# Four changes to a transformer kernel on one core: a column maximum by transposes, merged values in weight rooms, bias tiles opened earlier, expert gates applied to the activations

## The chip, the core and the metric

The kernel runs on one core of a Trainium2 chip. The metric is the device time of one launch in microseconds (us); lower is better. The core has a matrix engine (TensorE, PE in the profile), a vector engine (VectorE, DVE), a scalar engine (ScalarE, ACT), a general engine (GpSimd, POOL) and a queue engine (SyncE, SP), each of which runs its own list of instructions in order and waits on semaphores set by the others. On-chip memory is SBUF; matrix products land in a small accumulator memory, PSUM, which PE writes and DVE and ACT read. Everything here is in 32-bit floats unless said otherwise.

## The reference

The input is x of 2 x 1024 tokens by 256, and a context of 2 x 77 by 256. Four layers follow; each is an attention over the context and a feed-forward part, each with a layer norm before it and a residual after it:

- layer 0: 16-head attention, then eight dense 256x256 experts of which the gate keeps two;
- layer 1: 16-head attention, then an int8 matrix product;
- layer 2: one-head attention with a norm, then eight gated experts of width 128, of which two count;
- layer 3: 16 heads of width 64 with rotary positions and a relative bias, then eight experts with 320 places each, and a shared path for tokens that found no place.

The parts that the change touches are these lines (shortened):

```python
# layer 1: int8 product; the scale of rhs is one number per column
rhs_scale = maximum(max(abs(rhs), axis=0), 1e-12) / 127
q_rhs = clip(round(rhs / rhs_scale), -127, 127)
x = x + (q_lhs @ q_rhs) * lhs_scale * rhs_scale
# layer 2: eight experts, combined with the gate's weights
for e in range(8):
    o = silu(xf @ gate_proj[e].T) * (xf @ up_proj[e].T) @ down_proj[e].T
    y = y + combine_w[:, e, None] * o
# layer 3: bias by distance, values, output projection
scores = Q @ K.T * scale + rel_pos_bias[:, |i - j|]
x = x + (softmax(where(mask, scores, -1e9)) @ V) @ Wo
```

## The kernel before

The 2048 tokens are four groups (G) of 512, and each group is four slices (J) of 128 tokens, one per partition. x stays in SBUF throughout. The stages run in this order: attention 0 (names ending in a0), feed-forward 0 (f0), attention 1 (a1), then for each group the int8 product (f1) and attention 2 (a2) as a list of nine steps called `chain`, feed-forward 2 (f2), attention 3 (a3) and feed-forward 3 (f3). The chain of groups 0 and 1 is called from within attention 1 (function `beside`), that of groups 2 and 3 from within the loops of f2 over groups 0 and 1. The preparation of attention 3 is a generator, `layer3_setup`, whose pieces are also called between the pieces of f2.

The order of the source is not the order on the engines. A planner, which simulates the program as it is built, may move an instruction ahead of others on its engine as long as data and buffers allow; SP, which issues nearly all DMAs, and POOL are in order at run time like the other engines. So an instruction that waits holds all behind it on its engine.

Large matrices live in six rooms of 8 KB per partition, used in turn (`weight`, pool "w"). A matrix is loaded when the last reader of the room's former tenant is done. PSUM is used through two double-bank tiles (`pbig`) and some single-bank ones.

**Int8 matrix (`layer1_ffn_setup`, L577 to L587).** The 256x256 matrix rhs is loaded into a room at the start, and POOL takes the maximum of its absolute values over all partitions with `partition_all_reduce` (L580). DVE takes the larger of the two halves (L582), scales it (L583), inverts it (L584), and `quantize` (L567 to L573) rounds the matrix. In POOL's list L580 stands in the middle of attention 0, between multiplies by 1/sum of the softmax (L419).

**Feed-forward 2 (`layer2_ffn`, L692 to L770).** `route` computes a group's gate weights cw, 128 tokens by 8 experts per slice. `hidden` makes one expert's activations for 512 tokens: eight PE instructions of gate and up (L745, pgu_f; a 32-bit product is two PE instructions), silu on ACT (L750), and the product with up on DVE (L751, hT_f). `down` multiplies a slice's activations by the eight down matrices (L758), each expert into its own part of PSUM, and DVE adds each to x times its gate (L765): eight such evictions of 128x256 per slice, 128 in all.

**Attention 3 (`layer3_setup`, `layer3_attention`, L795 to L1012).** The values are merged with the output projection: each of 8 pieces (two batches by four key heads) is computed in PSUM, copied to a tile vo3 by ACT and DVE, and written to a DRAM tensor vd3 (L877 is its DMA). `layer3_attention` opens its own pools when those of f2 are closed, loads the rotary tables cs (L888), reads the merged values back as vw (L897, L900), and for each of 16 slices loads a bias tile rb of 128 x 16 x 77 (L920), adds the mask to it on POOL (L924), makes queries (L930, pq_a), rotates them (L781, L785 on DVE, L791 on POOL), transposes them (L949), makes scores (L965), adds the bias (L972), and after the softmax transposes the weights (L1000) and multiplies by vw (L1007).

**Feed-forward 3.** Tokens are scattered by indirect DMAs on POOL to a DRAM buffer by expert and place. The experts' matrices w1 and w2 (1 MB each) are loaded into the six rooms (L1317, L1319).

Of the kernel before, what the change touches and what calls it, by code (L numbers as in the profile page):

```python
# [33 lines left out]
P = 128  # L34
# [32 lines left out]
def tile_layers(ctx: ExitStack, tc: tile.TileContext, a: dict, out: bass.AP):  # L67
# [71 lines left out]


# [354 lines left out]
    def layer0_ffn(mp):  # L495
# [16 lines left out]
        for g in range(G):  # L512
# [19 lines left out]
            for j in range(J):  # L532
                nc.tensor.transpose(pg[:, j * P : (j + 1) * P], gate[:, j, :], ident)
# [41 lines left out]
    def layer1_ffn_setup():  # L575
# [4 lines left out]
        nc.gpsimd.partition_all_reduce(am, rw, P, bass_isa.ReduceOp.absmax)  # L580
        rsc, rrs = room[:, 0, 2], room[:, 0, 3]
        nc.vector.tensor_tensor(rsc, am[:, 0, :], am[:, 1, :], ALU.max)  # L582
        nc.vector.tensor_scalar(rsc, rsc, 1e-12, 1.0 / 127.0, ALU.max, ALU.mult)  # L583
# [108 lines left out]
    def layer2_ffn_weights():  # L692
        wgu = []
        for nm in ("gate2T", "up2T"):
            t = weight([P, KC, E * INTER], nm)
            nc.sync.dma_start(t, a[nm].rearrange("(c p) n -> p c n", p=P))
            wgu.append(t)
        return wgu

    def layer2_ffn(fp, wgu):  # L700

        wd = weight([P, E, D], "down2T")
        nc.sync.dma_start(wd, a["down2T"].rearrange("e i h -> i e h"))
# [3 lines left out]
        xnTs, cws, hTs = {}, {}, {}  # L707

        def route(g):
# [18 lines left out]
            cws[g] = cw = st.tile([P, J, E], F32, tag="cw", name=f"cw_{n}")  # L728
# [5 lines left out]
            nc.vector.tensor_tensor(cw, cw, bc(tot, E), ALU.mult)  # L734

        def hidden(g, e):
            n = f"f2{g}"
            if e % 4 == 0:
                hTs[g, e // 4] = fp.tile(
                    [P, E // 2, GT], F32, tag="hT", name=f"hT_{n}{e}", bufs=3  # L740
                )
            pgu = pbig(f"pgu_{n}{e}")
            for i in range(2):
                for kc in range(KC):
                    nc.tensor.matmul(  # L745
                        pgu[:, i, :], wgu[i][:, kc, e * INTER : (e + 1) * INTER],
                        xnTs[g][:, kc, :], start=(kc == 0), stop=(kc == KC - 1),
                    )
            sg = fp.tile([P, GT], F32, tag="sg", name=f"sg_{n}{e}")
            nc.scalar.activation(sg, pgu[:, 0, :], AF.Silu)  # L750
            nc.vector.tensor_tensor(hTs[g, e // 4][:, e % 4, :], sg, pgu[:, 1, :], ALU.mult)  # L751

        def down(g, j):
            x = xs[g][:, j, :]
            for half in range(2):
                po = pbig(f"po_f2{g}{j}{half}")
                for e in range(4):
                    nc.tensor.matmul(  # L758
                        po[:, e // 2, (e % 2) * D : (e % 2) * D + D],
                        hTs[g, half][:, e, j * P : (j + 1) * P], wd[:, 4 * half + e, :],  # L760
                        start=True, stop=True,
                    )
                for e in range(4):
                    ee = 4 * half + e
                    nc.vector.scalar_tensor_tensor(  # L765
                        x, po[:, e // 2, (e % 2) * D : (e % 2) * D + D],
                        cws[g][:, j, ee : ee + 1], x, ALU.mult, ALU.add,
                    )

        return route, hidden, down  # L770


# [22 lines left out]
    def layer3_setup():  # L795
# [67 lines left out]
        for b, vT in enumerate(vTs):  # L863
            vd = dp.tile([H * L, D], F32, name=f"vd3{b}")
            for g4 in range(KV):
                rows = slice(g4 % 2 * HD3, g4 % 2 * HD3 + HD3)
                vo = ap.tile([L, H // KV, D], F32, tag="vo3", name=f"vo3{b}{g4}")
# [14 lines left out]
        yield wq, mb3, kblk, vds  # L882

    def layer3_attention(route, wq, mb3, kblk, vds):
        with tc.tile_pool(name="a3", bufs=2) as ap, tc.tile_pool(name="a3c", bufs=1) as c3:
            cs = c3.tile([P, 2, 2, J, HD3], F32, name="cs")
# [6 lines left out]
            vws = []  # L893
            for b, vd in enumerate(vds):
                vw = c3.tile([P, NC3, D], F32, name=f"vw3{b}")
                full = (NC3 - 1) * P
                nc.sync.dma_start(  # L897
                    vw[:, : NC3 - 1, :], vd[:full, :].rearrange("(m p) n -> p m n", p=P)
                )
                nc.sync.dma_start(vw[: H * L - full, NC3 - 1, :], vd[full:, :])  # L900
                vws.append(vw)
# [14 lines left out]
            def queries(it):  # L916
                g, j = divmod(it, J)
                n, gb = f"a3{g}{j}", g % 2
                rb = ap.tile([P, H, L], F32, tag="rb", name=f"rb_{n}")
# [70 lines left out]
            def values(it):  # L990
# [15 lines left out]
                for m, w in chunks:  # L1006
                    nc.tensor.matmul(  # L1007
                        po, t[:w, m, :], vws[g // 2][:w, m, :], start=(m == 0), stop=(m == NC3 - 1)
                    )
# [350 lines left out]
    with tc.tile_pool(name="masks", bufs=1) as mp:  # L1360
# [13 lines left out]
        with (  # L1374
# [4 lines left out]
            def beside(it):  # L1379
# [4 lines left out]
                for g in range(2):  # L1384
                    k = it - (g + 1) * J + 1
                    if 0 <= k < len(chain):
                        chain[k](g)

# [8 lines left out]
            gate_up = layer2_ffn_weights()  # L1397
            layer1_attention(weights, beside)
            with tc.tile_pool(name="a3s", bufs=2) as sp, tc.tile_pool(name="f2", bufs=2) as fp:
                route, hidden, down = layer2_ffn(fp, gate_up)  # L1400
                setup.send(sp)


                route(0)
                for g in range(G):
                    pieces = [lambda e=e: hidden(g, e) for e in range(E)]
                    pieces += [lambda j=j: down(g, j) for j in range(J)]
                    for k, piece in enumerate(pieces):
# [84 lines left out]
```

## Time and profile before

| | |
|---|---|
| median of 3 runs | 1149.47 us (1144.49 to 1151.27) |
| profiled execution | 1150.59 us, its span 1148.7 us |
| mean granted PE clock | 0.952 of full |
| PE, DVE, ACT, POOL busy | 1029.8, 719.4, 362.1, 386.3 us |
| DMA moved | 74.89 MB, 65 GB/s on average |
| chain that ended last | PE 56%, DVE 24%, DMA 7%, ACT 4%, POOL 4% |

The stages overlap; by PE's first and last instruction of each they lie about at: a0 0 to 175 us, f0 157 to 310, a1 283 to 460, f2 462 to 709, a3 709 to 925, the end of the routing 925 to 952, f3 952 to 1149.

A row of the profile's timeline gives the start, the duration, the engine, the source line, the operation, output and inputs by the program's names, sizes, and in brackets how long the engine had been idle and what released it. "issue" there means that the engine waited for nothing that the profile shows. A row of the groups gives busy us, mean ns of one instruction, and the idle time before it with its releaser. The slices cut the span in 40 parts of 28.7 us; digits are tenths.

### The profile page before, as it was taken

The page shows a single profiled execution, that of the slowest core. Times are in us where ns is not written, and L with a number is a line of the kernel's source. Part 1 is how long each engine was busy: PE and PEld are TensorE (multiplying, and loading weights), DVE is VectorE, ACT ScalarE, POOL GpSimd, SP SyncE. Part 2 cuts the span into 40 slices and gives each one's busy share as a digit, 9 for nine tenths or more (in the row PEclk, how much of TensorE's full clock was granted, in tenths as well). Part 3 has the DMA queues.
Part 4 walks back from the last instruction along what each step waited for, and adds up shares of the span by engine and source line. Part 5 has one row for each costly group of instructions (what it writes and reads, how often), then busy time and mean ns, then how long its engine had stood idle before and what let it go on. Part 6 is the DMA issues. An engine that isn't in the chain of part 4 may idle for free.

```text
span 1148.7 us, 13916 instructions
## 1 busy us (share of the span) xinstructions
PE 1029.8 (90%) x4770; PEld 645.5 (56%) x4770; DVE 719.4 (63%) x1848; ACT 362.1 (32%) x1115; POOL 386.3 (34%) x368
## 2 busy tenths in 40 slices
PE   5499999999998987897998999899899958999996
PEld 3255554444444444455655546577678844766774
DVE  5567965776578898949586547677878731222211
ACT  1457640000076563131231110555355521111100
POOL 5443320112343544423120000675566641121211
PEclk9699998999999898898999999999999987999998
DMA  8400008245200000111102004523042323253630
GB/s 269 57 3 1 1 23 165 38 82 88 80 1 1 1 1 1 39 48 31 40 23 59 1 1 161 145 45 67 23 103 51 90 83 96 77 165 101 200 131 17
DMA packets 100279, 74.89 MB, mean 65 GB/s; under 512 B 57916, under 2 KB 90476, under 8 KB 100206
## 3 DMA queue, kind: packets, MB, share of 16 engines
q1 hardware_dynamic: 92974, 58.20, 18.3%
q10 hardware_dynamic: 4800, 9.46, 4.8%
q0 software_dynamic: 2432, 6.31, 1.6%
q8 instruction: 40, 0.66, 0.2%
q14 instruction: 33, 0.27, 0.1%
HBM read 55.35 MB, written 19.64 MB: 65 GB/s over the span
## 4 chain that ended last, share of the span: by engine, by line
PE 56%; DVE 24%; DMA 7%; ACT 4%; issue 4%; POOL 4%; SPq 0%; POOLq 0%; DVEq 0%; ACTq 0%
PE pe_f L545 10%; PE pgu_f L745 8%; PE poe_e L1273 4%; PE ph_e L1253 4%; PE po_a L1007 4%; DMA out_x<-ye_e,ids_e 3%; PE pq_a L930 3%; DVE x L765 3%; PE pc_a L450 3%; DVE x L156 2%; PE po_f L758 2%; PE pPT_a L437 2%; DVE mx_a L410 2%; DMA xe_e<-buf 2%; DVE sm_a L417 2%
## 5 line engine op out<-in xcount | busy, mean ns | idle before, releaser
L412 ACT ACTIVATE s_a<-psc_a,mx_a 128x77 f32<-128x77 f32 x512 | 121.5, 337 | 58.5 <-DVE mx_a L410 52.1
L419 POOL TENSOR_TENSOR s_a<-s_a,sm_a 128x616 f32<-128x616 f32 x64 | 78.3, 1223 | 123.9 <-DVE sm_a L418 89.4
L545 PE MATMUL pe_f<-ew,xnT_f 128*128 128x512 f32 x256 | 117.1, 607 | 0.0
L551 DVE SCALAR_TENSOR_TENSOR x<-pe_f,gate_f,x 128x256 f32<-128x256 f32 x128 | 61.8, 483 | 43.3 <-PE pe_f L545 40.7
L981 ACT ACTIVATE s_a<-s_a,mx_a 128x77 f32<-128x77 f32 x256 | 67.2, 347 | 61.4 <-DVE mx_a L979 61.2
L545 PEld LDWEIGHTS pe_f<-ew,xnT_f 128*128 128x128 f32 x256 | 48.3, 195 | 55.0 <-issue 53.0
L1007 PE MATMUL po_a<-vw,PT_a 128*128 128x256 f32 (+1 forms) x320 | 77.3, 381 | 0.8 <-ACT PT_a L1002 0.8
L1253 PE MATMUL ph_e<-xT_e,w 128*128 128x320 f32 x256 | 75.6, 436 | 0.0
L758 PE MATMUL po_f<-down2T,hT_f 128*128 128x256 f32 x256 | 65.0, 400 | 8.8 <-DVE x L765 8.7
L437 PE MATMUL pPT_a<-cst,s_a 128*128 128x128 f32 (+1 forms) x320 | 55.0, 292 | 17.8 <-POOL vr_a L343 11.5
L410 DVE TENSOR_REDUCE mx_a<-psc_a 128x4 f32<-128x308 f32 x128 | 57.9, 466 | 18.6 <-PE psc_a L401 11.4
L1077 DVE TENSOR_SCALAR hT_e<-ph_e,b1c 128x320 f32<-128x320 f32 (+1 forms) x36 | 20.6, 572 | 75.3 <-PE ph_e L1253 75.3
L930 PE MATMUL pq_a<-wq,xnT_a 128*128 128x512 f32 x128 | 60.5, 610 | 4.7 <-DVE s_a L972 4.7
L745 PE MATMUL pgu_f<-xnT_f,gate2T 128*128 128x512 f32 x128 | 63.5, 619 | 1.0 <-DVE hT_f L751 0.6
L765 DVE SCALAR_TENSOR_TENSOR x<-po_f,cw_f,x 128x256 f32<-128x256 f32 x128 | 60.8, 480 | 5.7 <-PE po_f L758 2.5
L437 PEld LDWEIGHTS pPT_a<-cst,s_a 128*128 128x128 f32 (+1 forms) x320 | 35.9, 143 | 49.5 <-issue 17.9
L1007 PEld LDWEIGHTS po_a<-vw,PT_a 128*128 128x128 f32 (+1 forms) x320 | 57.8, 190 | 9.6 <-issue 1.4
L1075 ACT ACTIVATE hT_e<-ph_e,b1c 128x320 f32<-128x320 f32 (+1 forms) x36 | 19.6, 545 | 138.0 <-PE ph_e L1253 138.0
L1273 PE MATMUL poe_e<-w,hT_e 128*128 128x256 f32 x256 | 61.3, 381 | 0.0
L758 PEld LDWEIGHTS po_f<-down2T,hT_f 128*128 128x128 f32 x256 | 48.3, 197 | 22.7 <-DVE x L765 15.4
L450 PE MATMUL pc_a<-PT_a,vblk_a 128*32 128x256 f32 (+1 forms) x512 | 57.2, 400 | 4.2 <-DVE PT_a L445 2.2
L745 PE MATMUL pgu_f<-xnT_f,up2T 128*128 128x512 f32 x128 | 60.1, 592 | 0.0
(311 smaller groups left out, 1979.8 us busy)
## 6 DMA issues: line engine op xcount, KB each, us to landing
w<-in_L_ffn_w SPq DMA_DIRECT2D x16, 1024.0 KB
rb_a<-in_relbias SPq DMA_DIRECT2D x16, 616.0 KB
buf<-none ACTq DMA_DIRECT2D x12, 769.5 KB
vd<-vo SPq DMA_DIRECT2D x8, 308.0 KB
vw<-vd SPq DMA_DIRECT2D x2, 1152.0 KB
xe_e<-buf SPq DMA_DIRECT2D x8, 257.0 KB
x<-in_x SPq DMA_DIRECT2D x4, 512.0 KB
ew<-in_L_ffn_expert_w SPq DMA_DIRECT2D x4, 512.0 KB
```

Source lines behind the costliest of these rows:

```text
L410: nc.vector.tensor_reduce(mx, sv, AX.X, ALU.min)
L412: nc.scalar.activation(s[:, c, 4 * i + h, :], sv[:, h, :], AF.Exp, bias=mx[:, h : h + 1], scale=-1.0,)
L437: nc.tensor.transpose(pt[: wide(m), m - m0, k * P : (k + 1) * P], sp[k][:, c, m * P : m * P + wide(m)], ident,)
L450: nc.tensor.matmul(pc[cols, c, :], vblk[g // 2][: wide(m), c, m, cols], t[: wide(m), m, :], start=(k == 0), stop=(k == 1),)
L545: nc.tensor.matmul(pe[:, i, :], xnT[:, kc, j * P : (j + 1) * P], ew[half][:, kc, i * 512 : (i + 1) * 512], start=(kc == 0), stop=(kc == KC ...
L745: nc.tensor.matmul(pgu[:, i, :], wgu[i][:, kc, e * INTER : (e + 1) * INTER], xnTs[g][:, kc, :], start=(kc == 0), stop=(kc == KC - 1),)
L758: nc.tensor.matmul(po[:, e // 2, (e % 2) * D : (e % 2) * D + D], hTs[g, half][:, e, j * P : (j + 1) * P], wd[:, 4 * half + e, :], start=Tr ...
L765: nc.vector.scalar_tensor_tensor(x, po[:, e // 2, (e % 2) * D : (e % 2) * D + D], cws[g][:, j, ee : ee + 1], x, ALU.mult, ALU.add,)
L930: nc.tensor.matmul(pq[:, i, :], xnTs[g][:, kc, j * P : (j + 1) * P], wq[:, kc, i * 512 : (i + 1) * 512], start=(kc == 0), stop=(kc == KC - 1),
L1007: nc.tensor.matmul(po, t[:w, m, :], vws[g // 2][:w, m, :], start=(m == 0), stop=(m == NC3 - 1))
L1253: nc.tensor.matmul(ph[:, h % 2, :rows], w1[:, kc, h * P : (h + 1) * P], xT[:, kc, :], start=(kc == 0), stop=(kc == KC - 1),)
L1273: nc.tensor.matmul(po, hT[:, h, i * P : (i + 1) * P], w2[:, h, :], start=(h == 0), stop=(h == NH - 1),)
```

## The change

Four parts, which share the SBUF and the rooms that they free or take.

1. **Maximum by transposes.** `partition_all_reduce` goes. PE transposes the matrix in four blocks, not before the gate transposes of f0's group 1 have been issued (`issue_after(gated[1])`); DVE takes the absolute maximum along the free axis and scales it; the result, copied along 128 columns, is transposed back by PE and copied by ACT.
2. **Merged values in weight rooms.** vw3 is no longer a tile of attention 3's pool: three weight rooms take its 18 chunks. They are loaded at the end of `layer3_setup`, that is, during f2. vo3 has one buffer instead of two.
3. **Bias tiles beside f2.** The pool of the bias tiles (a3c) is opened before f2's pools, so the first two tiles do not wait for f2's memory. In SP's list the loads of the first two stand right behind csk and m3; their mask additions stand in POOL's list among the first layer-2 attention steps of f2. The rotary tables move to the pool that opens after f2.
4. **Gates in the activations.** In f2, for groups 1 to 3, the gate weights are transposed by PE, copied by ACT, written to DRAM and read back once per expert as a tile cb in which all partitions hold the row of 512 gates. POOL multiplies silu's output by cb before DVE multiplies by up. The down products of all eight experts then accumulate in one PSUM tile, and DVE adds it to x once per slice. Group 0 keeps the former way. Its `route` is called from `beside`, and the loads of the router move with it.

With three rooms held by vw3 until attention 3 has used them, the first two experts' matrices of f3 are loaded later: w1_0 stands in SP's list between the bias loads rb_a322 and rb_a323, w2_0 before rb_a333, w1_1 behind it, w2_1 before the first load of tokens for f3.

```diff
+    gated = {}
...
-                nc.tensor.transpose(pg[:, j * P : (j + 1) * P], gate[:, j, :], ident)
+                turn_gate = nc.tensor.transpose(pg[:, j * P : (j + 1) * P], gate[:, j, :], ident)
+            gated[g] = turn_gate.ins
...
-        nc.gpsimd.partition_all_reduce(am, rw, P, bass_isa.ReduceOp.absmax)
         rsc, rrs = room[:, 0, 2], room[:, 0, 3]
-        nc.vector.tensor_tensor(rsc, am[:, 0, :], am[:, 1, :], ALU.max)
-        nc.vector.tensor_scalar(rsc, rsc, 1e-12, 1.0 / 127.0, ALU.max, ALU.mult)
+        pt = pturn("prhs").rearrange("n (c k) -> n c k", c=KC)
+        with tc.issue_after(gated[1]):
+            for c in range(KC):
+                for kc in range(KC):
+                    nc.tensor.transpose(
+                        pt[:, c, kc * P : (kc + 1) * P], rw[:, kc, c * P : (c + 1) * P], ident
+                    )
+        top = room[:, 1, 3, :KC]
+        nc.vector.tensor_reduce(top, pt, AX.X, ALU.max, apply_absolute_value=True)
+        nc.vector.tensor_scalar(top, top, 1e-12, 1.0 / 127.0, ALU.max, ALU.mult)
+        nc.vector.tensor_copy(am[:, :, :P], bc(top, P))
+        pb = pturn("prsc")[:, :D]
+        for c in range(KC):
+            nc.tensor.transpose(pb[:, c * P : (c + 1) * P], am[:, c, :P], ident)
+        nc.scalar.copy(rsc, pb)
         nc.vector.reciprocal(rrs, rsc)
...
             nc.vector.tensor_tensor(cw, cw, bc(tot, E), ALU.mult)
+            if g == 0:
+                cws[g] = cw
+                return
+            pc = pside(f"pcw_{n}")[:E, :]
+            for j in range(J):
+                nc.tensor.transpose(pc[:, j * P : (j + 1) * P], cw[:, j, :], ident)
+            cwT = st.tile([E, J, P], F32, tag="gT", name=f"cwT_{n}", bufs=2)
+            cwT = cwT.rearrange("e j p -> e (j p)")
+            nc.scalar.copy(cwT, pc)
+            cwds[g] = cwd = dp.tile([E, GT], F32, name=f"cwd_{n}")
+            nc.sync.dma_start(cwd, cwT)
...
+                if e == 0 and g > 0:
+                    for i in range(E):
+                        cbs[i] = fp.tile([P, GT], F32, tag="cb", name=f"cb_{n}{i}", bufs=5)
+                        nc.sync.dma_start(cbs[i], cwds[g][i, :].partition_broadcast(P))
...
+                if g > 0:
+                    nc.gpsimd.tensor_tensor(sg, sg, cbs[e], ALU.mult)
...
+                po = pone(f"po_f2{g}{j}")[:, :D]
+                for e in range(E):
                     nc.tensor.matmul(
+                        po, hTs[g, e // 4][:, e % 4, j * P : (j + 1) * P], wd[:, e, :],
+                        start=(e == 0), stop=(e == E - 1),
                     )
+                nc.vector.tensor_tensor(x, x, po, ALU.add)
...
-                vo = ap.tile([L, H // KV, D], F32, tag="vo3", name=f"vo3{b}{g4}")
+                vo = ap.tile([L, H // KV, D], F32, tag="vo3", bufs=1, name=f"vo3{b}{g4}")
...
+        rooms = [weight([P, 8, D], f"vw3{i}") for i in range(-(-NB * NC3 // 8))]
+        vws = [[rooms[c // 8][:, c % 8] for c in range(b * NC3, (b + 1) * NC3)] for b in range(NB)]
+        for b, vd in enumerate(vds):
+            m = 0
+            while m < NC3 - 1:
+                c = b * NC3 + m
+                n = min(8 - c % 8, NC3 - 1 - m)
+                nc.sync.dma_start(
+                    rooms[c // 8][:, c % 8 : c % 8 + n],
+                    vd[m * P : (m + n) * P, :].rearrange("(m p) n -> p m n", p=P),
+                )
+                m += n
+            nc.sync.dma_start(vws[b][m][: H * L - m * P], vd[m * P :, :])
...
-            cs = c3.tile([P, 2, 2, J, HD3], F32, name="cs")
+            cs = ap.tile([P, 2, 2, J, HD3], F32, name="cs", bufs=1)
...
-                rb = ap.tile([P, H, L], F32, tag="rb", name=f"rb_{n}")
+                rb = c3.tile([P, H, L], F32, tag="rb", name=f"rb_{n}", bufs=2)
...
+                if it == J + len(chain):
+                    route(0)
...
-            with tc.tile_pool(name="a3s", bufs=2) as sp, tc.tile_pool(name="f2", bufs=2) as fp:
-                route, hidden, down = layer2_ffn(fp, gate_up)
-                setup.send(sp)
-                route(0)
+            with tc.tile_pool(name="a3c", bufs=1) as c3:
+                with tc.tile_pool(name="a3s", bufs=2) as sp, tc.tile_pool(name="f2", bufs=2) as fp:
+                    hidden, down = units(fp)
+                    setup.send(sp)
```

## The prediction

> **What bounds the kernel now.** I read the page's busy rows and slices first, then TensorE's timeline for idle stretches over 0.6 us, then what each waited for.
>
> ```profile
> PE 1029.8 (90%) x4770; PEld 645.5 (56%) x4770; DVE 719.4 (63%) x1848; ACT 362.1 (32%) x1115; POOL 386.3 (34%) x368
> ...
> PE   5499999999998987897998999899899958999996
> ...
> PEclk9699998999999898898999999999999987999998
> ...
> L419 POOL TENSOR_TENSOR s_a<-s_a,sm_a 128x616 f32<-128x616 f32 x64 | 78.3, 1223 | 123.9 <-DVE sm_a L418 89.4
> ...
> L758 PE MATMUL po_f<-down2T,hT_f 128*128 128x256 f32 x256 | 65.0, 400 | 8.8 <-DVE x L765 8.7
> ...
> L765 DVE SCALAR_TENSOR_TENSOR x<-po_f,cw_f,x 128x256 f32<-128x256 f32 x128 | 60.8, 480 | 5.7 <-PE po_f L758 2.5
> ```
>
> TensorE (PE) is busy 90% of a span of 1148.7 us. So the change can win only where PE stands idle, or runs at the half clock that shows in PEclk behind such an idle. The first two slices (0 to 57 us) and the routing before the last experts (slice 33) are the large holes. PE's idle stretches over 0.6 us sum to 85.6 us; the longest is in the start:
>
> ```profile
> 42.93 1.95 POOL L580 PARTITION_ALL_REDUCE rhs<-rhs  x1 [7.06 <-DVE sm_a L417]
> 52.52 1.21 POOL L419 TENSOR_TENSOR s_a<-s_a,sm_a 128x616 f32<-128x616 f32 x1 [7.63 <-issue]
> 53.70 2.49 POOL L355 TENSOR_TENSOR vblk_a<-vr_a,cst 128x640 f32<-128x640 f32 x2
> 56.16 1.21 POOL L419 TENSOR_TENSOR s_a<-s_a,sm_a 128x616 f32<-128x616 f32 x1
> ```
>
> The all-reduce of the int8 weight shows 1.95 us, but POOL then stands 7.63 us with nothing awaited ("issue") before it takes up the softmax multiply whose input (the reciprocal at 43.03 on DVE) was long there. PE's transposes of that softmax begin at 57.41 behind an idle of 11.52 us.
>
> **The change part by part.** All times are of the profiled execution (1150.59 us, of which the span is 1148.7; the median of the runs is 1149.47, so 1.1 less).
>
> *All-reduce replaced.* Without L580 the multiply starts at 43.2 (reciprocal 43.03 + 0.15) and takes 1.21; the two vblk products follow at 44.4 and take 2.49 (their DMA was issued by 39.6, and POOL took them without a DMA wait); the next multiply ends at 48.1. PE restarts about 48.2 instead of 57.41: −9.2. Ends: −5 if DVE (4.0 of 4.0 us busy from 46 to 50) becomes next, −12 with the clock below.
>
> [...] Row: granted clock 1.00 in 42 to 46 us, 0.50 from 50 to 62; the four pq_a at 58.75 take 3.62 us, the same four at 70.72 take 1.88. [...] The idle left, 45.9 to 48.2, is 2.3 us. [...]
>
> The replacement moves into the layer-0 feed-forward: four PE transposes (0.11 each when back to back, as po_a's neighbours L1000 show: four in 0.60 with the fill), an absmax reduce of 128x512 from PSUM (as L181's 0.68), two small DVE operations and a copy of 128x256 (about 0.7), two transposes, an ACT copy (0.4), then the reciprocal 1.74 and quantize's four (0.68, 0.42, 0.88, 1.38) which already existed. DVE is half idle there (L551, 8 matmuls of 3.44 us against four evictions of 0.48), so these 6 us are covered; PE pays 0.7 and can wait for a turn in DVE's queue: +1.5 (0 to +4). The result is first read about 80 us later.
>
> *Gates into the activations, groups 1 to 3 of the third feed-forward.* It removes 96 of L765's 128 evictions, 96 × 0.48 = 46 us of DVE, and adds 12 additions (0.48 each by the same row, 6 us), 24 POOL products 128x512, 12 transposes, 3 ACT copies, 3 DRAM writes and 24 broadcast loads of 256 KB. DVE's saving counts only where DVE set PE's pace:
>
> ```profile
> 632.00:647.00 15.00, 15.00 (x37) 6.81 (x36) 2.75 (x4) 2.57 (x5) 0.00 (x0) 1.00 0.00 0
> 647.00:664.00 17.00, 16.08 (x71) 12.01 (x70) 15.32 (x36) 0.89 (x2) 0.00 (x0) 1.00 0.00 0
> ...
> 692.00:709.00 17.00, 16.10 (x73) 12.13 (x71) 14.56 (x30) 1.00 (x2) 0.00 (x0) 1.00 0.33 120
> ```
>
> (Columns: window, its length, busy us and count of PE, weight loads, DVE, ACT, POOL, then granted clock, DMA.) The hidden halves are full of PE work; the down halves hold 64 matmuls of 0.217 = 13.9 plus 0.9 of transposes, and take 17.2: 2.4 to 3.4 lost per group. Three groups: −8. The new transposes cost PE 3 × 0.44, and I take 1 in all: −7 (−12 to +5).
>
> What hides the products: an expert's two matrices keep PE 3.46 us and two PSUM rooms allow 6.9 for one round; silu 0.7, POOL 1.02 (L419's 1.223 × 512/616), DVE 0.67 and semaphores make 6.3 with the matmuls. Without that 0.6 us of cover PE waits per expert. What hides the gates' way through DRAM in group 1: behind the transposes PE has three blocks of work and two experts, about 9.6 us, against ACT copy 0.7 + write and broadcast of about 2.7 us each (the rope tables issued at 709.07 had landed by 712.7) = 6; groups 2 and 3 have 12 or more.
>
> [...]
>
> ```profile
> 471.43 2.40 POOL L685 TENSOR_TENSOR o_a<-o_a,r_L_xattn_gamma 128x1024 f32<-128x1024 f32 x1 [2.08 <-DVE o_a L156]
> ```
>
> ```profile
> 471.53 2.33 DVE L211 TENSOR_TENSOR eq_f20g<-gs_f 128x16 f32<-128x16 f32 x1
> ```
>
> A 0.16 us comparison lasts as long as the POOL operation. [...] By the row, were every product to hold DVE, 24 × 1.02 = 24. I take 0 (groups 2 and 3 have DVE half idle) and keep 24 for the range.
>
> *Bias tiles opened beside this stage.* The two first additions (L924, 2.59 each) move from 724 to 732 to about 470 to 480, in the middle of those comparisons, in POOL's queue between gamma and the x addition. hT_f200 and then PE's pk stand behind them:
>
> ```profile
> 476.85 1.99 PE L822 MATMUL pk<-wkv,ctxT 128*77 128x256 f32 x4 [5.34 <-DVE hT_f L751]
> ```
>
> One further lock of 2.6 lengthens this idle: +2.7 (0 to +5).
>
> *Merged values in weight rooms.* Their loads (2.4 MB between 710 and 717) leave the border between third feed-forward and last attention; the single vo3 tile makes its next copy wait about 2 us for a DMA, behind 3.5 us of PE work. At the border itself
>
> ```profile
> 728.16 4.11 PE L930 MATMUL pq_a<-wq,xnT_a 128*128 128x512 f32 x5 [3.90 <-DVE s_a L972]
> ```
>
> is PE waiting for a late bias tile; that goes. But PE now takes two of the first three pq before the last po, and the rope tables still wait for that po: landing 2.7, then DVE's rope 1.23 + 1.28 before the third pq has a room: 5.2 us idle. The same work later ends about 1 us later: +1 (−3 to +4; half clock follows either idle, as the 0.82 us per matmul here shows).
>
> *Expert weights later.* w1_0 (1 MB) now stands in SP's queue ahead of rb_a323. It waits for a product done at 842.4, and rb_a323 goes at 845.2, so issue is not late, but 3 us of transfer (up to 364 GB/s at 690) is ahead of it. POOL's additions:
>
> ```profile
> 849.53 2.58 POOL L924 TENSOR_TENSOR rb_a<-rb_a,mb 128x1232 f32<-128x1232 f32 x1 [1.26 <-DMA rb_a<-in_relbias]
> 854.68 2.36 POOL L791 TENSOR_TENSOR q_a<-q_a,r_a 128x1024 f32<-128x1024 f32 x1 [2.57 <-DVE r_a L785]
> ```
>
> have 2.57 us of slack before q_a, which PE's transposes need: +0.5 (0 to +6). w1_1 and w2_1 now move in 921 to 940 beside the last scatters: +1 (0 to +3).
>
> Sum: −9.2 −1.5 +1.5 −7 +2.7 +1 +0.5 +1 = −11.0, hence 1139.6 against the profiled 1150.59, about 1139 against the median.
>
> **Rivals.**
> 1. *Only one of the two gains arrives.* DVE or ACT limits the start after 48 us, or the down halves stay at 17 us because the gated chain is late. For: ACT and DVE are busy in 46 to 50. Against: both idle 7.7 us before 58. −11 + 7 or + 6: about 1145.
> 2. *More than forecast.* The moved additions meet no comparison, the rope tables land before they matter: −11 −2.7 −3 −2 (half clocks after those idles) = 1131.
> 3. *POOL becomes the brake, slower.* Place: groups 1 to 3, POOL's products. Price: up to 24 × 1.02 us, when each holds DVE or stands in POOL's order behind the layer-2 attention's gamma and x additions (2.40 + 2.17). Point: the chain's 0.6 us of cover; from 11 products fully exposed on, the gain is gone; with 19 it is 1139 + 19 = 1158. For: the 471.53 row. [...]
>
> **How the numbers follow.** Forecast 0.50 (own range 1133 to 1145), rival 1 0.19, rival 2 0.12, rival 3 0.19. Runs of this kernel (1144.49 to 1151.27) tell 0.5%, 5.7 us, from no change: same is 1143.7 to 1155.2. Faster: 0.44 of the first, 0.06 of rival 1, 0.12 = 0.62. Same: 0.06 + 0.13 = 0.19. Slower 0.19. The range reaches into rivals 2 and 3: 1127 to 1159.
>
> **What would show it.** Right: the PE idle near 46 under 3 us and clock 1.0 after it; the down halves of groups 1 to 3 without idle; no bias wait near 724, a rope wait instead. Wrong: PE waiting for hT in groups 1 to 3 with POOL's product named, PE waiting for pcw or a cb load, or the 471 idle grown by over 5 us.

## The result and the profile after

The changed kernel takes 1152.89 us (median of 20 runs, 1147.97 to 1157.6) against 1148.68 us of the kernel before (20 runs taken with it, 1144.49 to 1152.29): a ratio of 1.0034, 95% interval 1.0024 to 1.0045. It is 0.34%, some 4 us, slower. That is less than the 0.5% that the prediction set as its bound of no change, and on the other side of the forecast of 1139. The profiled execution took 1153.57 us, its span 1151.8 (before 1150.59 and 1148.7).

The page's busy row and slices of the changed kernel:

```profile
PE 1032.7 (90%) x4788; PEld 648.2 (56%) x4788; DVE 694.6 (60%) x1765; ACT 367.6 (32%) x1121; POOL 415.3 (36%) x391
...
PE   5899989999997887697798999899899967999996
...
PEclk9899989999998998788999999899999977999998
```

DVE lost 25 us of work and POOL gained 29, and PE, which bounds the kernel, has 3 us more in a span 3 us longer. The second slice rose from 4 to 8 with its clock from 6 to 8: the start is repaired. Lower than before by one or two digits are, among others, slices 13 and 14 (attention 1), 17 (the start of f2's group 0) and 20 (the down products at the end of group 0). Where on PE's timeline it went, by the start (first row) or the end of the same instruction in both traces (us; attention 3 ends at 931.60, not at 925 as the list of stages above has it):

| place | before | after | difference |
|---|---|---|---|
| second softmax's transposes, attention 0 | 57.41 | 45.74 | −11.7 |
| last expert product of f0 | 310.08 | 299.65 | −10.4 |
| last output product of attention 1 | 459.81 | 453.82 | −6.0 |
| last gate and up product of f2's group 0 | 513.62 | 517.31 | +3.7 |
| last output product of attention 3 | 931.60 | 934.89 | +3.3 |
| end of the span | 1148.69 | 1151.80 | +3.1 |

So 11.7 us are won in the first 46 us; 4.4 are lost in attention 1, where the diff touches nothing, and 9.7 in the first of four groups of f2. From there to the end gains and losses nearly cancel.

**The start.** PE's timeline of the kernel before, 57 to 62 us (columns: start, duration, engine, line, operation, operands, count; in brackets the idle time before it and what ended it):

```profile
57.41 1.54 PE L437 MATMUL pPT_a<-cst,s_a 128*128 128x128 f32 x6 [11.52 <-POOL vr_a L343]
58.75 3.62 PE L374 MATMUL pq_a<-xnT_a,w_a 128*128 128x512 f32 x4
```

POOL's timeline of the changed kernel, 36 to 46 us, and PE's, 45 to 52 us:

```profile
39.95 1.22 POOL L421 TENSOR_TENSOR s_a<-s_a,sm_a 128x616 f32<-128x616 f32 x1 [3.59 <-DVE sm_a L420]
41.12 2.51 POOL L357 TENSOR_TENSOR vblk_a<-vr_a,cst 128x640 f32<-128x640 f32 x2
43.86 1.22 POOL L421 TENSOR_TENSOR s_a<-s_a,sm_a 128x616 f32<-128x616 f32 x1 [0.23 <-DVE sm_a L420]
```

```profile
45.02 0.79 PE L403 MATMUL psc_a<-kblk_a,qT_a 64*128 64x308 f32 x4
45.74 0.88 PE L439 MATMUL pPT_a<-cst,s_a 128*128 128x128 f32 x6
...
49.97 1.88 PE L376 MATMUL pq_a<-xnT_a,w_a 128*128 128x512 f32 x4
```

The multiply that stood at 52.52 behind 7.63 us of "issue" now stands at 39.95, POOL's operations at 41.12 and 43.86 follow it with 0.23 us of idle, and the idle of 11.52 us ahead of PE's transposes is gone, with the half clock behind it (granted 0.50 from 50 to 62 us, 3.62 us for four matmuls; now granted 1.00 from 42 to 62, 1.88).

**Group 0 of f2.** PE's, POOL's and DVE's timelines of the changed kernel, 455 to 480 us:

```profile
473.83 1.99 PE L868 MATMUL pk<-wkv,ctxT 128*77 128x256 f32 x4 [8.30 <-DVE hT_f L785]
...
479.24 3.75 PE L777 MATMUL pgu_f<-xnT_f,gate2T 128*128 128x512 f32 x4 [1.28 <-DVE gt_f20g L215]
```

```profile
463.49 2.59 POOL L976 TENSOR_TENSOR rb_a<-rb_a,mb 128x1232 f32<-128x1232 f32 x1
...
468.01 2.40 POOL L701 TENSOR_TENSOR o_a<-o_a,r_L_xattn_gamma 128x1024 f32<-128x1024 f32 x1 [1.93 <-DVE o_a L158]
470.37 2.61 POOL L976 TENSOR_TENSOR rb_a<-rb_a,mb 128x1232 f32<-128x1232 f32 x1
```

```profile
463.56 2.68 DVE L574 TENSOR_SCALAR x<-x,lrs_f 128x256 f32<-128x256 f32 x1
...
468.11 2.33 DVE L213 TENSOR_TENSOR eq_f20g<-gs_f 128x16 f32<-128x16 f32 x1
470.44 2.57 DVE L213 TENSOR_TENSOR eq_f20g<-gs_f 128x16 f32<-128x16 f32 x1
```

Each mask addition has a DVE operation beside it that starts within 0.1 us of it and ends with it: a 128x256 one-input operation that lasts 2.68 us at 463.56 (0.34 in most places), and a comparison, 0.16 us elsewhere, that lasts 2.57 at 470.44. The wait of PE for hT, 5.34 us before, is 8.30, and the matmuls at 479.24 run at half clock (granted 0.50; 3.75 us for four, 1.88 elsewhere).

**The border to attention 3.** PE's timeline of the kernel before, 728 to 734 us:

```profile
728.16 5.40 PE L930 MATMUL pq_a<-wq,xnT_a 128*128 128x512 f32 x8 [3.90 <-DVE s_a L972]
```

PE's, the SP queue's and DVE's timelines of the changed kernel, 717 to 731 us:

```profile
724.05 6.21 PE L982 MATMUL pq_a<-wq,xnT_a 128*128 128x512 f32 x8 [6.56 <-DVE r_a L831]
```

```profile
717.52 0.89 SPq L949 DMA_DIRECT2D cs<-in_ropeq  x2
```

```profile
720.44 2.36 DVE L827 TENSOR_TENSOR q_a<-pq_a,cs 128x1024 f32<-128x1024 f32 x2 [2.50 <-DMA cs<-in_ropeq]
722.72 1.28 DVE L831 TENSOR_TENSOR r_a<-pq_a,cs 128x512 f32<-128x512 f32 x2
```

The rope tables are issued when f2's pools close, land at 720.4, and PE's third pq waits behind DVE's rope for a room: 6.56 us idle, then 6.21 us for eight matmuls that took 3.60 at 704.83 (granted clock 0.50 from 724.05 to 729.1, 1.00 at 704.83). The wait for a late bias tile of the kernel before (3.90 us idle, 5.40 for the eight matmuls, granted 0.50 from 728.7 to 732.0) is gone; this one stands in its place and costs 3.5 us more. The kernel before loads the tables behind f2 too (L888 at 709.07): the change gives them another pool, not a later place.

### The profile page after: what moved, and what is told of

It reads as the page before. It is cut to its first block, busy times and chain, and to the rows that moved or that the text cites. A ratio compares the mean times of both kernels' runs of the same rounds, so it can differ in the third digit from the quotient of the medians.

```text
span 1151.8 us, 13951 instructions
## 1 busy us (share of the span) xinstructions
PE 1032.7 (90%) x4788; PEld 648.2 (56%) x4788; DVE 694.6 (60%) x1765; ACT 367.6 (32%) x1121; POOL 415.3 (36%) x391
## 4 chain that ended last, share of the span: by engine, by line
PE 60%; DVE 20%; DMA 9%; ACT 3%; POOL 3%; issue 3%; SPq 1%; POOLq 0%; DVEq 0%; ACTq 0%
PE pe_f L548 10%; PE pgu_f L777 8%; PE poe_e L1325 4%; PE pq_a L982 4%; PE po_a L1059 4%; DMA out_x<-ye_e,ids_e 3%; PE pc_a L452 3%; PE ph_e L1305 3%; PE pPT_a L439 3%; DVE x L158 3%; PE po_f L808 2%; DMA xe_e<-buf 2%; PE psc_a L403 2%; PE pq_a L376 2%; PE psc_a L1017 2%
## 5 line engine op out<-in xcount | busy, mean ns | idle before, releaser
L1305 PEld LDWEIGHTS ph_e<-xT_e,w 128*128 128x128 f32 x256 | 47.5, 190 | 18.8 <-issue 3.1
L419 DVE TENSOR_REDUCE sm_a<-s_a 128x8 f32<-128x616 f32 x64 | 50.3, 786 | 12.5 <-ACT s_a L414 11.0
L785 DVE TENSOR_TENSOR hT_f<-sg_f,pgu_f 128x512 f32<-128x512 f32 x32 | 21.8, 681 | 59.2 <-POOL sg_f L784 46.9
```

The lines of the kernel that those rows point to most:

```text
L1305: nc.tensor.matmul(ph[:, h % 2, :rows], w1[:, kc, h * P : (h + 1) * P], xT[:, kc, :], start=(kc == 0), stop=(kc == KC - 1),)
```

## The experiments

My first theory, out of the two traces: four causes in different places. Part 1 is a gain of its own, less a cost in attention 1; the early mask additions hold DVE in group 0; the late rope tables cost the border; the gates in the activations gain little. The rival for each was that the loss belongs to the gates of f2, or to part 1's work itself.

**Part 1 alone.** The kernel before with the transposes in place of the all-reduce; nothing else.

```diff
-        nc.gpsimd.partition_all_reduce(am, rw, P, bass_isa.ReduceOp.absmax)
+        with tc.issue_after(gated[1]):
+            # transposes, reduce, transposes back, copy: as in the change
```

> The kernel before with the maximum by transposes alone. Its order on every engine equals the changed kernel's up to the end of attention 1, and the former kernel's from there on. Theory (the other parts lose what this one wins): faster than before by about 6 us, ratio 0.995, with the end of attention 1 near 453.8 us as in the changed kernel. Rival (the lead of 12 us at the start would have lasted; attention 1 lost 4.4 us to the other parts): 10 us faster, ratio 0.991.

1143.58 us, ratio 0.9935 (0.9923 to 0.9948), span 1141.5. The lead is 11.9 at the second softmax, 11.2 at the end of f0, 7.5 at the end of attention 1, 8.0 after attention 3. So part 1 alone carries the gain and the 3.7 us loss in attention 1; the loss has nothing to do with the other three parts.

**Bias tiles late.** The changed kernel with the bias tiles in attention 3's own pool again, so that loads and mask additions stand where they stood.

```diff
-                rb = c3.tile([P, H, L], F32, tag="rb", name=f"rb_{n}", bufs=2)
+                rb = ap.tile([P, H, L], F32, tag="rb", name=f"rb_{n}")
```

> The changed kernel with the bias tiles back in the pool that opens after the third feed-forward. Theory (the two mask additions on POOL cost group 0 of that stage 8 to 10 us): group 0 ends 8 us earlier than in the changed kernel; at the border both rope tables and bias tiles are now late, so 3 to 5 us are given back: 1147 to 1150 us, faster than the changed kernel by 3 to 6. Rival (group 0 lost to the earlier routing or to the order of PE): group 0 ends as late as in the changed kernel, and the time is 1153 to 1157.

1146.54 us, 0.9957 (0.9944 to 0.997), span 1145.2: 6.6 us faster than the changed kernel by the spans and a little more than the theory had. At the last gate and up product of group 0 the lead over the kernel before is 8.6 us, where the change trails by 3.7.

**Mask additions held.** The tiles and their early loads stay as changed; only POOL's two additions are put behind the last gate product of group 1.

```diff
-                    nc.gpsimd.tensor_tensor(sg, sg, cbs[e], ALU.mult)
+                    held[g, e] = nc.gpsimd.tensor_tensor(sg, sg, cbs[e], ALU.mult).ins
...
+                with tc.issue_after(held[1, 7]):
                     nc.gpsimd.tensor_tensor(
                         rb, rb, mb3[:, g // 2, :].unsqueeze(1).to_broadcast([P, H, L]), ALU.add
                     )
```

> The changed kernel, bias tiles loaded early as there, with only their two mask additions held on POOL behind the last gate product of group 1. Theory (the additions lock DVE in the middle of the layer-2 routing): group 0 loses nothing against the kernel before, 8 us less than the changed kernel: about 1144 us. Rival (early loads, memory or the moved routing cost, not the additions): within 2 us of the changed kernel.

1146.31 us, 0.996 (0.9946 to 0.9974), span 1144.6. PE's and POOL's timelines of this run at the place of the loss:

```profile
469.73 1.99 PE L868 MATMUL pk<-wkv,ctxT 128*77 128x256 f32 x4 [5.76 <-DVE hT_f L785]
...
473.65 2.79 PE L777 MATMUL pgu_f<-xnT_f,gate2T 128*128 128x512 f32 x4
```

```profile
464.31 2.40 POOL L701 TENSOR_TENSOR o_a<-o_a,r_L_xattn_gamma 128x1024 f32<-128x1024 f32 x1 [2.08 <-DVE o_a L158]
466.79 2.17 POOL L704 TENSOR_TENSOR x<-x,o_a 128x1024 f32<-128x1024 f32 x1
```

With the two additions gone from between them, gamma and the x addition stand back to back, and the wait for hT is 5.76 again. PE's list is the same in this run and in the changed kernel up to 494 us. There the changed kernel trails by 1.6 us ahead of the wait for hT and by 9.3 at the end: two POOL additions of 2.6 us each cost 7.7 us at this place, and 7.2 of the span (6.6 by the medians). The early tiles and loads cost nothing that shows.

**Rope tables early.** On top of the late bias tiles, the tables move to the pool that is open beside f2, so they are loaded earlier than in either kernel.

```diff
-            cs = ap.tile([P, 2, 2, J, HD3], F32, name="cs", bufs=1)
+            cs = c3.tile([P, 2, 2, J, HD3], F32, name="cs", bufs=1)
```

> As the run with late bias tiles, but the rope tables take their place in the pool opened before the third feed-forward. Theory (the rope tables, not the place of the pq matmuls, make the idle of 6.6 us at the border): against that run 3 to 6 us less, since only the bias wait of about 4 us stays; 1141 to 1146 us. Rival (PE's order at the border costs, whatever lands): no difference from that run.

1139.84 us, 0.9896 (0.988 to 0.9911), span 1138.4: 6.7 us under the run with late bias tiles. PE's timeline of that run, and of this one, at the border:

```profile
715.79 6.17 PE L982 MATMUL pq_a<-wq,xnT_a 128*128 128x512 f32 x8 [6.72 <-DVE r_a L831]
```

```profile
711.36 3.70 PE L982 MATMUL pq_a<-wq,xnT_a 128*128 128x512 f32 x8 [2.92 <-DVE r_a L831]
```

The idle falls from 6.72 to 2.92 us and the eight matmuls behind it take 3.70 us instead of 6.17: 6.3 us, nearly the whole difference. PE's lists of the two runs differ at 16 places, all at the border. The span is 3.2 us under that of part 1 alone, but that run loads its tables late, like the kernel before, so not all of this is the change's.

**Two vo3 tiles.** The same with the second buffer of the merged values, in case its copies waited.

```diff
-                vo = ap.tile([L, H // KV, D], F32, tag="vo3", bufs=1, name=f"vo3{b}{g4}")
+                vo = ap.tile([L, H // KV, D], F32, tag="vo3", name=f"vo3{b}{g4}")
```

> The run with late bias tiles and early rope tables, with two vo3 tiles instead of one. Theory (the single tile's wait is hidden behind PE's work): within 1 us of that run. Rival (the wait of DVE's copy for the DMA delays hT): 1 to 3 us faster.

1143.84 us, 0.9947 (0.9932 to 0.9962), with a profiled execution of 1140.28 and a span of 1138.5, as without the buffer. The other timed runs lie 3 to 4 us above the profiled one and nothing in the trace tells why. Neither expectation came true: nothing here speaks for a gain, and the loss stays open.

**Old gates.** The run with early rope tables, with all four groups of f2 weighted by DVE as before.

```diff
-            if g == 0:
-                cws[g] = cw
-                return
+            cws[g] = cw
+            return
...
-                if g > 0:
-                    nc.gpsimd.tensor_tensor(sg, sg, cbs[e], ALU.mult)
...
-                if g == 0:
+                if True:
```

> The run with late bias tiles and early rope tables, with the gates of all groups applied by DVE as before. Theory (the gates in the activations win about 6 us in groups 1 to 3 net of what POOL's products cost): 4 to 8 us slower than that run, 1144 to 1148. Rival (nothing won there, the border gives it all): equal to that run within 2 us.

1139.39 us, 0.9904 (0.9889 to 0.9919), span 1138.9. The main expectation failed: with the gates or without, the time is the same within the noise. The gain that I had taken at 7 us is about zero net.

**Gates for groups 2 and 3 only.** Group 1 is weighted by DVE too.

```diff
-            if g == 0:
+            if g < 2:
...
-                if g > 0:
+                if g > 1:
                     nc.gpsimd.tensor_tensor(sg, sg, cbs[e], ALU.mult)
```

> The run with late bias tiles and early rope tables, gates in the activations for groups 2 and 3 only. In group 1 the layer-2 attention of the last group shares POOL and DVE, and small DVE operations of the routing last 1.2 to 2.3 us beside POOL's products and additions. Theory (POOL's products in group 1 cost as much as the evictions they spare): within 2 us of that run, with the idle of 4 us before pw gone. Rival (no such cost): slower by the 2.5 to 3.4 us of a down half.

1137.2 us, 0.9892 (0.9877 to 0.9907), span 1134.2. By the medians, whose intervals overlap, groups 2 and 3 gain 2.2 against the old gates and group 1's gates cost 2.6; by the spans, 4.7 and 4.2. But 1.6 of the 4.7 stands already at the end of f0, where no gate has been applied, so 3.1 is left. Sum of four windows of this run, from 611 to 686 us (columns as in the prediction's windows):

```profile
sum 75.00, PE 75.00 PEld 42.71 DVE 18.15 ACT 11.16 POOL 21.50; mean PE 18.75 PEld 10.68 DVE 4.54 ACT 2.79 POOL 5.38
```

PE has no idle left in 75 us, at a clock of 1.00: what the gates were meant to do, they do where DVE has little but hT and additions. There was not much to win: in the run with the old gates PE is busy 89.96 of the 92.00 us of these two groups. In group 1 it is otherwise. PE's, POOL's and DVE's timelines of the run with gates in all three groups (late bias tiles, early rope tables), 574 to 589 us:

```profile
584.91 3.69 PE L916 MATMUL pw<-wo,vT 64*77 64x256 f32 x8 [4.05 <-DVE hT_f L785]
```

```profile
574.77 2.35 POOL L701 TENSOR_TENSOR o_a<-o_a,r_L_xattn_gamma 128x1024 f32<-128x1024 f32 x1 [1.50 <-DVE o_a L158]
577.08 1.26 POOL L784 TENSOR_TENSOR sg_f<-sg_f,cb_f 128x512 f32<-128x512 f32 x1
578.30 2.18 POOL L704 TENSOR_TENSOR x<-x,o_a 128x1024 f32<-128x1024 f32 x1
580.43 1.26 POOL L784 TENSOR_TENSOR sg_f<-sg_f,cb_f 128x512 f32<-128x512 f32 x1
```

```profile
574.86 2.29 DVE L218 TENSOR_SCALAR m_f22g<-rank_f22g 128x16 f32<-128x16 f32 x1
577.19 1.20 DVE L737 TENSOR_TENSOR ch_f<-ch_f,m_f22g 128x32 f32<-128x32 f32 x1
578.42 2.13 DVE L212 TENSOR_TENSOR gt_f<-ch_f 128x64 f32<-128x64 f32 x1
580.48 1.30 DVE L213 TENSOR_TENSOR eq_f<-ch_f 128x64 f32<-128x64 f32 x1
```

POOL takes gamma, a product, the x addition and a product without a pause, and DVE's routing operations for group 2 advance one per POOL operation: four of them in 7 us, each 0.15 to 0.21 us where POOL is quiet. The two products hold 2.1 of the 6.2 us that are lost so, gamma and the x addition the rest. The hT product stands behind them in DVE's list, and PE waits 4.05 us and then takes 3.69 us for eight matmuls, 1.95 elsewhere. Without group 1's gates this wait is gone, but DVE's list has another order there too, with hT products between the routing operations; what of the loss is the products' and what the order's was not separated.

The changed kernel itself does not show this wait. Its additions have delayed group 0, gamma and the x addition fall at 594.29 and 596.73, and PE's only idle over 0.6 us in group 1 is 1.30.

**The all-reduce moved.** The kernel before with its `partition_all_reduce` kept, but queued on POOL behind the last softmax multiply of attention 0.

```diff
-        nc.gpsimd.partition_all_reduce(am, rw, P, bass_isa.ReduceOp.absmax)
+        with tc.issue_after(held["a0"]):
+            nc.gpsimd.partition_all_reduce(am, rw, P, bass_isa.ReduceOp.absmax)
```

> The kernel before with its partition_all_reduce kept, but queued on POOL behind the last softmax multiply of attention 0. In attention 0 its order is that of the run with the transposes alone, in attention 1 that of the kernel before. Theory (the four us lost in attention 1 come from the planner's new order there): attention 1 keeps the whole lead, about 11 us at its end instead of 7.5, and the time is 4 us under the run with the transposes alone, about 1140. Rival (the lead shrinks in attention 1 whatever its order, since something there waits for a fixed rate of DVE or ACT): 7 to 8 us at the end of attention 1 and the same time as that run, 1143 to 1145.

1153.12 us, 1.0031 (1.0016 to 1.0045), span 1149.8: both expectations failed. POOL's and PE's timelines of this run, 150 to 185 us:

```profile
157.70 1.95 POOL L583 PARTITION_ALL_REDUCE rhs<-rhs  x1 [5.95 <-issue]
170.16 0.52 POOL L1043 MEMSET none<- 128x512 f32 x1 [10.50 <-PE po_a L461]
...
170.66 0.12 POOL L345 MEMSET vr_a<- 128x32 f32 x1
179.17 0.25 POOL L151 TENSOR_SCALAR rstd_f<-mv_f 128x4 f32<-128x4 f32 x1 [8.39 <-issue]
```

```profile
182.76 1.02 PE L535 MATMUL pgT_f<-cst,gate_f 128*8 128x128 f32 x4 [9.79 <-DVE x L542]
```

The start of attention 0 gains its 11.7 us, and the whole of it is lost again between 157 and 183: PE is idle for 3.88 us, behind DVE operations that want the result, and for 9.79. POOL waits for nothing in the 5.95 us ahead of the operation. Behind it three memsets run when PE's product is there, and only then, ahead of the first operation that reads SBUF (L151, of a layer norm that PE needs), come 8.39 us of "issue"; in the changed kernel, which has no all-reduce, the same L151 behind the same memsets stands at 165.62 and waits 1.29 us. So the cost is the operation's own in both places tried, and here its second half begins at 170.8, 11 us behind the end of its record of 1.95 us. This run also tells of attention 1: its PE order there is the order of the kernel before, and the stage, from the last expert product of f0 to the last output product, takes 149.9 us (before 149.7, part 1 alone 153.4, changed 154.2).

**Other PSUM rooms for part 1.** Part 1 alone has the planner write attention 1 in another order (238 places of PE's list differ from before). To tell that order from the new work, the same instructions take the routing's PSUM room, which gives a third order.

```diff
-        pt = pturn("prhs").rearrange("n (c k) -> n c k", c=KC)
+        pt = pside("prhs").rearrange("n (c k) -> n c k", c=KC)
...
-        pb = pturn("prsc")[:, :D]
+        pb = pside("prsc")[:, :D]
```

> The kernel before with part 1 alone, as in the run of part 1 alone (span 1141.5), but the two groups of transposes use the PSUM room of the routing instead of the rooms of the turns. The orders of attention 0 and of f2 to the end are those of that run (but for three places in f2's group 0); f0 has its few transposes at other places, and attention 1 has another order, nearer to that of the kernel before (123 places of PE's list differ, against 238). Theory that attention 1's order took the 4 us: attention 1, from the last expert product of f0 to its last output product, takes 150 to 151 instead of 153.4, and the span is 1137 to 1139. Rival that part 1 itself costs attention 1 its 4 us (through the transposed matrix, its late quantization or the memory of it): 153 to 154 again, span 1141 to 1143.

1139.95 us, 0.9912 (0.988 to 0.9943), span 1138.2. Attention 1 takes 150.15 us (296.09 to 446.24), against 153.4. Sums over 150 us of attention 1, from about its start, first of part 1 alone and then of this run:

```profile
sum 150.00, PE 128.12 PEld 68.13 DVE 125.73 ACT 84.80 POOL 65.43; mean PE 21.35 PEld 11.36 DVE 20.96 ACT 14.13 POOL 10.91
```

```profile
sum 150.00, PE 131.45 PEld 71.26 DVE 127.35 ACT 86.77 POOL 66.03; mean PE 21.91 PEld 11.88 DVE 21.23 ACT 14.46 POOL 11.00
```

The same instructions in another order keep PE busy 3.3 us longer in the same time. The end of f0 comes 2.8 us earlier as well, and some 2 us are lost again behind attention 3. Attention 1 is now within 0.4 us of the kernel before, with all of part 1's work in place: the 3.7 us came with the order that the former room brought, not with the work. Which wait of that order costs them was not found.

**All that was found, together.** Late bias tiles, early rope tables, gates in groups 2 and 3, and the other PSUM rooms.

```diff
-        pt = pturn("prhs").rearrange("n (c k) -> n c k", c=KC)
+        pt = pside("prhs").rearrange("n (c k) -> n c k", c=KC)
...
-                if g > 0:
+                if g > 1:
...
-            cs = ap.tile([P, 2, 2, J, HD3], F32, name="cs", bufs=1)
+            cs = c3.tile([P, 2, 2, J, HD3], F32, name="cs", bufs=1)
...
-                rb = c3.tile([P, H, L], F32, tag="rb", name=f"rb_{n}", bufs=2)
+                rb = ap.tile([P, H, L], F32, tag="rb", name=f"rb_{n}")
```

> The changed kernel with late bias tiles, early rope tables and gates in the activations for groups 2 and 3 only (1137.2 before), with the same other PSUM room for part 1's transposes. If attention 1's order took 4 us: about 1134 (span 1131 to 1132). If part 1 itself costs them: 1137. The order of f2 differs at some 120 places as well, which may move either by 2 us.

1132.41 us (1131.26 to 1133.39), 0.985 (0.9819 to 0.9881), span 1129.3: faster than both kernels, and 4.8 us under the same without the other rooms, where the theory of the order had 3.

## Why the prediction was wrong

The forecast was 11.0 us faster; the profile shows 3.1 slower. Of the 14.1 between them 6.5 are the gates, whose POOL products I let hold nothing on DVE; 4.5 the mask additions, counted as one hold of two and without the half clock; 3.2 the work of part 1, with attention 1 taken as unchanged; 1.1 the border; the start won 1.2 more than I took.

The spans of the runs, each a step from its neighbour, close the account: before 1148.7, part 1 alone 1141.5 (−7.2); with merged values, late expert weights and early rope tables 1138.9 (−2.6); with gates in groups 1 to 3 1138.4 (−0.5); with the rope tables late 1144.6 (+6.2, here with the bias tiles early and their additions held); with the additions in group 0 1151.8 (+7.2). The sum is +3.1; mine was −11.0. It is one path through the parts: on another the same part has another price, since the wait in group 1 that the gates cost in the runs with late bias tiles is not there in the changed kernel.

| step of the prediction | said | measured |
|---|---|---|
| all-reduce replaced, with the clock | −10.7 | −11.6 to −12.7 (−11.9 in part 1 alone) |
| its replacement in f0, all of part 1 after that | +1.5 | +4.7 (f0 0.8, attention 1 3.7) |
| gates, groups 1 to 3 | −7 | −0.5 |
| early mask additions | +2.7 | +7.2 |
| border, merged values, expert weights | +2.5 | +3.6 (−2.6 and +6.2) |

*Start: right in cause, in size partly by chance.* The bound was POOL's unexplained idle. The sum of its rows gave −9.2 at the transposes and −10.7 with the clock behind them. The transposes already stand 11.7 us earlier, ahead of any effect of the clock: the multiply comes at 39.95, not at my 43.2. It is the second of attention 0, and DVE's second reciprocal stands at 39.13 in the kernel before; the one at 43.03, from which I reckoned, is the third's. So the all-reduce, ahead of it in POOL's list, held it from 39.3 on. The −1.5 for the clock was an estimate of mine that no run shows; in its place the changed kernel showed no idle over 0.3 us left, a granted clock of 1.00 from 42 to 62 us, 1.88 us for the pq at 49.97, and the next pq at 57.08 for 70.72: a lead of 13.6, 2.0 more than at the transposes. At the first expert product of f0 the lead is 11.7 again; what takes the 2 us back in attention 0 was not found, and that the total came so near to −10.7 is luck. I had counted only POOL's idle behind the all-reduce; the one ahead of it, 7.06 us put down to DVE's sum (L417), may have been its own in part as well: moved, the operation had 5.95 us ahead of it with no wait at all. That isn't shown for the start, where the order of attention 0 changed too.

*Attention 1: a step that was missing.* I counted what moved on the engines around the new instructions and took stages that the diff doesn't touch as unchanged. The planner's order of attention 1 as written for the changed kernel is another one than before, and that can be read without a run. Its direction could not have been told from it; 4 us either way belonged in the range.

*Gates: half to two thirds of the size in two groups and the sign wrong in one.* By the sum's own shares groups 2 and 3 were to win 4.6 and win 2 to 3. Group 1 was to win 2.3 and loses 2.6 by the medians, 4.2 by the spans. The step that failed is the 0 that I took for what the products hold of DVE. hT and the new additions are not held where they meet a product in the changed kernel (hT at 630.11 takes 0.67 us beside one of 1.40, two additions at 667.35 take 0.74 beside one of 1.28), but the routing comparisons ahead of hT in DVE's list are, as the four of 1.20 to 2.29 us from 574.86 to 581.78 in the run with late bias tiles and early rope tables show, and hT stands behind them. This is rival 3 at the place that it named, among gamma and the x addition; my 0 was taken from groups 2 and 3, where DVE is half idle and the windows show 0.00 for POOL. The product was also longer than its scaled row:

```profile
688.93 1.27 POOL L784 TENSOR_TENSOR sg_f<-sg_f,cb_f 128x512 f32<-128x512 f32 x1 [3.89 <-ACT sg_f L782]
```

This line of the changed kernel has 1.27 us, where I scaled 1.22 us of a 128x616 multiply to 1.02; so the cover of 0.6 us per expert was 0.35.

*Early mask additions: right mechanism, a term sized at little over a third.* "One further lock of 2.6 lengthens this idle: +2.7" counted one lock of the two, and only on the comparisons. The other, at 463.56, held an operation that I had not looked at (L574, of the quantization in the feed-forward before); and the half clock behind the idle, which I had priced at the border and not here, took 3.75 us for the first four gate products against 2.79 in the run with the additions held. The sign that I had named, the idle at 471 grown by over 5 us, was too coarse: it grew by 3.0.

*Border: right in sign and in its line, short in size.* A rope wait in place of a bias wait was forecast with 5.2 us idle and came with 6.56, since the tables landed 3 us into it and DVE turned both q blocks first. The half clock, which I had as equal behind either idle, is longer too: 6.21 us for eight matmuls where the kernel before has 5.40. Together 3.5 us, where I took 1; the 6.2 of the table is the price against tables loaded early, which neither kernel has. Expert weights cost little: POOL's bias addition at 854.18 waits 2.83 us for its DMA, before 1.26, and the slack ahead of q_a falls to 1.60:

```profile
854.18 2.77 POOL L976 TENSOR_TENSOR rb_a<-rb_a,mb 128x1232 f32<-128x1232 f32 x1 [2.83 <-DMA rb_a<-in_relbias]
...
858.54 2.37 POOL L837 TENSOR_TENSOR q_a<-q_a,r_a 128x1024 f32<-128x1024 f32 x1 [1.60 <-PE pxnT_f L177]
```

*What stays open.* The orders of f2 and attention 3 differ between some of these runs, so each entry holds an order's luck of a few us besides its cause. Bias tiles and rope tables both early, with the additions held, was not tried. The 4 us of the run with two vo3 tiles are unexplained.

## What to carry to other kernels

Before an operation is moved to POOL, ask what DVE has in its list at that moment, not only what consumes its result: in the changed kernel a comparison of 0.16 us lasted 2.57 beside an addition of 2.61, and PE's wait for the hT behind it in DVE's list rose from 5.34 to 8.30 us. The idle of POOL at `partition_all_reduce` belonged to that operation in both places tried: 7.63 us behind it in the kernel before; moved, 5.95 ahead of it and 8.39 ahead of L151, three memsets behind it. Where a planner writes the order, compare the orders of stages that the change doesn't touch. Try a second room or buffer for the new work before a loss is put down to it.

## What the runs showed of the hardware

- `partition_all_reduce` on 128x512 has a record of 1.95 us, with 7.06 us of idle before and 7.63 after it in the kernel before. Moved to 157.70, where it waited for nothing, it has 5.95 before it, and 8.39 stand ahead of L151, though three memsets had run in between.
- Two DVE operations of one input lasted as long as the POOL operation on two SBUF inputs beside them: in the changed kernel the 128x256 scaling (L574) took 2.68 us beside an addition of 2.59, 0.34 in most places; with late bias tiles and early rope tables the 128x16 comparison with a scalar (L218) took 2.29 beside gamma's 2.35 (0.15 to 0.17 in the changed kernel where POOL was quiet).
- A POOL multiply of 128x512 with a full second input took 1.26 to 1.27 us in the run with late bias tiles and early rope tables, a little longer than a 128x616 multiply by a broadcast reciprocal (1.22).
